# An attention kernel on one Trainium2 core: row maxima written to DRAM head by head, and read back by GpSimd with a stride of four elements

## The chip, the cores and the metric

The kernel runs on one core of a Trainium2 chip. A core has TensorE (PE, matrix products and transposes), VectorE (DVE), ScalarE (ACT), GpSimd (POOL) and SyncE (SP, which here only issues transfers), an on-chip memory SBUF of 128 partitions, an accumulation memory PSUM of eight banks, and sixteen DMA engines that move data between DRAM and SBUF. Each engine works off its own instructions in the order in which they were written; semaphores order the engines among each other.

The metric is the device time of one execution in microseconds (us), as the median of several runs.

## What is computed

One block of a transformer: attention over 16 heads of 8 channels with a bucket term, and a feed-forward network, each followed by a normalization and a residual sum. The input has 16 batches of 512 tokens of 128 channels, in f32.

```
def attention(x, Wq, bq, Wv, bv, hyperplanes):        # B=16, S=512, E=128, H=16
    q = (x @ Wq.T + bq).reshape(B, S, H, 8)
    v = (x @ Wv.T + bv).reshape(B, S, H, 8)
    bits = (concat([q, 1]) @ hyperplanes >= 0)         # 6 bits -> a bucket of 64
    buckets = sum(bits * 2 ** arange(6))
    scores = q @ q.T / sqrt(E)                         # per batch and head, 512 x 512
    same = buckets[:, None] == buckets[None, :]
    attn = softmax(scores * (62 + same), axis=-1)
    return attn @ v

x = x + layernorm(attention(layernorm(x)))
x = x + layernorm(ffn(layernorm(x)))                   # 128 -> 512 -> 512 -> 512 -> 128
```

Queries serve as keys, so scores times coefficient is a symmetric matrix: the maximum of row s is the maximum of column s.

## The kernel before

**Order.** All instructions are put into an order ahead of time by a small planner, `Order` (lines 47 to 187). The kernel is written as generators that yield steps such as `dve(cost, rank, emit)`, `pool(...)`, `act(...)`, `pe(...)` and `dma(kb, rank, emit)`; the planner holds a clock for each engine, and at each moment emits the ready step with the lowest rank. The costs in the code are its estimates in us. Buffers are handed out by `Pool` objects (lines 361 to 374), so a step that needs a buffer is emitted after the step that gives it back. Each engine's queue is then fixed, SP's with the transfers too.

**A head.** There are 16 x 16 = 256 heads j, each with a 512 x 512 matrix of logits, kept in one tile `l` of 128 partitions x 4 x 512. Row s = 128 t + p lies in partition p, part t. The steps are:

- `gather` (L821): three transfers on SP bring ql and qr (the queries, split into three bf16 parts) and bb (the buckets, repeated over all partitions). Four sets of these buffers exist.
- `scores` (L872) and `coeffs` (L889): four products on TensorE (L881) into three PSUM banks, four comparisons of buckets on VectorE (L899).
- `logits` (L913): four instructions on VectorE (L934), each multiplying scores by coefficients into `l` and leaving the maximum of each row in one column of a small tile. There are eleven buffers for `l`.
- `maxima` (L963): the maxima lie with one row in each partition, and are wanted as one line of 512 values in every partition. The tile that took them is one of two tiles `mxpads` of 128 x 32 f32 (lines 322 to 326). VectorE transposes it in blocks of 32 x 32 (L967), SP writes the result to a DRAM tile `md` (L972) in the order of the columns. From the fifth head on, two heads share one such tile, one transpose and one write (`MH = 2`); the first four heads go singly (`SINGLES = 4`).
- `softmax` (L977): SP loads the 512 maxima of the head into each of the 128 partitions (tile `mb`, L984, three buffers). GpSimd subtracts them from all four parts of `l` in one instruction over 2048 elements a partition (L991): here column c of every row has the maximum of row c subtracted, so the matrix becomes the transpose of the softmax's argument. ScalarE takes the exponential in place (L996).
- `attend` (L1040): for each four heads, TensorE multiplies by the values (L1056), which needs the matrix with the summed index in the partitions, hence the subtraction by columns.

Five heads (`BY_ROWS`, j = 3, 7, 11, 15, 19) go another way: ScalarE subtracts the row's maximum from within its exponential (L1007), and TensorE transposes afterwards. They don't use GpSimd, so it subtracts 251 times.

GpSimd also takes small powers for the normalizations (L469, L593), and two scalings of weights (L1369) at the start. The feed-forward network (`ffn`, L1139) of a batch runs among the heads of later batches: its products are L1208, L1252 and L1290, its activations L1196 and L1266 on ScalarE.

Of the kernel before, what the change touches and what calls it, by code (L numbers as in the profile page):

```python
# [13 lines left out]
F32 = mybir.dt.float32  # L14
BF16 = mybir.dt.bfloat16
AF = mybir.ActivationFunctionType
ALU = mybir.AluOpType
# [4 lines left out]
P = 128  # L22
# [168 lines left out]
def tile_lsh_attention_ffn(  # L191
# [20 lines left out]
    nc = tc.nc  # L212
    B, S, E = x.shape
    NH = hyper.shape[1]
    DH = hyper.shape[0] - 1
    H = E // DH
    HID = w1_t.shape[1]
    NT = S // P
    NC = HID // P
    GH = 4  # L220
    NG = H // GH
    Q = P // GH
# [5 lines left out]
    GROUPS = (1, 2, 6, B)  # L228
    LATE = 20
    COLD = 10.0  # L230
    SINGLES = 4
    SCALE = 1.0 / math.sqrt(E)
    AHEAD = 1
    MH = 2
    LB = 11
    BY_ROWS = (3, 7, 11, 15, 19)
    SLOTS = H * NT
# [2 lines left out]
    const = ctx.enter_context(tc.tile_pool(name="const", bufs=1))  # L240
    p1 = ctx.enter_context(tc.tile_pool(name="p1", bufs=1))
    p2 = ctx.enter_context(tc.tile_pool(name="p2", bufs=2))
    ps_b = ctx.enter_context(tc.tile_pool(name="ps_b", bufs=1, space=PSUM))
    dram = ctx.enter_context(tc.tile_pool(name="dram", bufs=2, space=DRAM))

    od = Order()
# [17 lines left out]
        out=hb_sb,  # L264
        in_=hyper[DH].unsqueeze(0).unsqueeze(2).to_broadcast([H, NH, 1]),
# [31 lines left out]
        op=ALU.mult,  # L297
# [16 lines left out]
    for i in range(2):  # L314
# [3 lines left out]
            va[:, :, 0 : H * DA].rearrange("p t (h d) -> p t h d", d=DA)[:, :, :, DH], 1.0  # L318
        )
        vaugs.append(va)  # L320

    mxpads = []
    for i in range(2):
        mp = const.tile([P, Q], F32, name=f"mxpad{i}")
        nc.vector.memset(mp, 0.0)
        mxpads.append(mp)
    bkts = []
    for i in range(2):
        bk = const.tile([H, BR, BP], BF16, name=f"bkt{i}")
# [6 lines left out]
    def pe(cost, rank, emit):  # L336
        return ("op", "PE", cost, emit, rank, None)

    def dve(cost, rank, emit):
        return ("op", "DVE", cost, emit, rank, None)  # L340

    def act(cost, rank, emit, table=None):
        return ("op", "ACT", cost, emit, rank, table)

    def pool(cost, rank, emit):
        return ("op", "POOL", cost, emit, rank, None)

    def dma(kb, rank, emit, held=True, cost=0.35):
        return ("dma", "SP", cost, emit, rank, None, kb, held)

    def get(kind):
        return ("get", kind)

    def wait(event):
        return ("wait", event)

    def events(n):
        return [Event() for _ in range(n)]
# [5 lines left out]
    logit_bufs = Pool("l", LB)  # L364
    row_bufs = Pool("r", 4)
    co_bufs = Pool("co", 4)
    mx_bufs = Pool("mx", 2)
    mb_bufs = Pool("mb", 3)
    row_mx_bufs = Pool("rx", 2)
    h_bufs = Pool("h", 3)  # L370
    x1_bufs = Pool("x1_", 2)
    xnt_bufs = Pool("xntf", 1)
# [11 lines left out]
    def bank(tag, name):  # L384
        return ps_b.tile([P, 512], F32, tag=tag, name=name)
# [525 lines left out]
                od.loose()  # L911

    def logits():  # L913
        pair = []
        for j in range(B * H):
            kl = yield get(logit_bufs)
            by_rows = j in BY_ROWS
            if by_rows:
                kr = yield get(row_mx_bufs)
                mx_, base = p1.tile([P, NT], F32, tag=kr, name=f"mx_{j}"), 0  # L920
            else:
                if not pair:
                    km = yield get(mx_bufs)
                    mx = mxpads[int(km[2:])]
                mx_, base = mx, len(pair) * NT
            l = p1.tile([P, NT, S], F32, tag=kl, name=f"l_{j}")
            for t in range(NT):
                i = j * NT + t
                yield wait(scored[i])
                yield wait(weighed[i])  # L930
                (sp, ks), (co, kc) = sps.pop(i), cos.pop(i)

                def emit(t=t + base, sp=sp, co=co, l=l[:, t, :], mx=mx_):
                    nc.vector.tensor_tensor_reduce(  # L934
                        out=l,
                        in0=co[:, 0:S],
                        in1=sp,
                        scale=1.0,
                        scalar=-3.0e38,
                        op0=ALU.mult,  # L940
                        op1=ALU.max,
                        accum_out=mx[:, t : t + 1],
                    )

                yield dve(0.61, 5, emit)
                od.put(score_banks, ks)
                od.put(co_bufs, kc)
                if t < NT - 1:
                    od.loose()
            od.put(row_bufs, rows.pop(j)[3])  # L950
            ls[j] = l, logit_bufs, kl
            if by_rows:
                od.spawn(softmax_by_rows(j, l, kl, mx_, kr))
            else:
                pair.append((j, l))
                if j < SINGLES or len(pair) == MH or j == B * H - 1:
                    od.spawn(maxima(pair, mx, km))
                    pair = []
            if j % GH == GH - 1:
                od.spawn(attend(j // GH))  # L960
            od.loose()

    def maxima(heads, mx, km):  # L963


        mt = p2.tile([P, Q], F32, tag="mt", name=f"mt_{heads[0][0]}")
        yield dve(0.14, 0, lambda: nc.vector.transpose(mt, mx))  # L967
        od.put(mx_bufs, km)

        md = dram.tile([Q, GH, Q], F32, tag="md", name=f"md_{heads[0][0]}", bufs=4)  # L970
        yield dma(
            16, 0, lambda: nc.sync.dma_start(out=md.rearrange("t k q -> k t q"), in_=mt), cost=0.6  # L972
        )
        for i, (j, l) in enumerate(heads):
            od.spawn(softmax(j, l, md[i * NT : (i + 1) * NT]))

    def softmax(j, l, md):  # L977

        km = yield get(mb_bufs)
        mb = p1.tile([P, S], F32, tag=km, name=f"mb_{j}")  # L980
        yield dma(
            256,
            0,
            lambda: nc.sync.dma_start(  # L984
                out=mb, in_=md.rearrange("t k q -> (t k q)").partition_broadcast(P)
            ),
        )
        yield pool(
            4.52,
            1,  # L990
            lambda: nc.gpsimd.tensor_tensor(  # L991
                l, l, mb.unsqueeze(1).to_broadcast([P, NT, S]), op=ALU.subtract
            ),
        )
        od.put(mb_bufs, km)
        yield act(1.82, 0, lambda: nc.scalar.activation(l, l, AF.Exp, scale=SCALE), "exp")  # L996
        od.set(exped[j])

    def softmax_by_rows(j, l, kl, mx, kr):


        nmx = p1.tile([P, NT], F32, tag="n" + kr, name=f"nmx_{j}")
        yield act(0.22, -5, lambda: nc.scalar.activation(nmx, mx, AF.Copy, scale=-SCALE))

        def weigh():
            for t in range(NT):
                nc.scalar.activation(  # L1007
                    l[:, t, :], l[:, t, :], AF.Exp, bias=nmx[:, t : t + 1], scale=SCALE
                )

        yield act(2.3, 0, weigh, "exp")
        od.put(row_mx_bufs, kr)
        kh = yield get(h_bufs)
        w = p1.tile([P, NT, S], F32, tag=kh, name=f"w_{j}")
        there = events(NT)

        def evict(t, tp, k):
            yield act(0.5, -2, lambda: nc.scalar.copy(w[:, t, :], tp))
            od.put(banks, k)
            od.set(there[t])  # L1020

        for t in range(NT):
            k = yield get(banks)
            tp = bank(k, f"tw_{j}_{t}")

            def turn(t=t, tp=tp):
                for i in range(NT):
                    nc.tensor.transpose(tp[:, ts(i, P)], l[:, i, ts(t, P)], ident)

            yield pe(0.45, 1, turn)  # L1030
            od.spawn(evict(t, tp, k))
        od.put(logit_bufs, kl)
        for e in there:
            yield wait(e)
        ls[j] = w, h_bufs, kh
        od.set(exped[j])
# [373 lines left out]
    with tc.manual_schedule():  # L1410
        for piece in (prep(0), gathers(), scores(), coeffs(), logits(), weights(), inputs(), activity()):
            od.spawn(piece)
        od.run()
# [52 lines left out]
```

## Time and profile before

| | us |
|---|---|
| median of 3 runs | 1368.63 (1368.58 to 1369.19) |
| the profiled execution, its own time | 1371.57 |
| its span, from first to last instruction | 1369.80 |
| first subtraction on GpSimd (L991) starts | 41.45 |
| last subtraction ends | 1295.23 |

The granted clock of TensorE was 0.989 of full speed over the span.

Some groups of instructions, in number, mean duration and the total of their busy time:

| line | engine | what | number | mean ns | busy us |
|---|---|---|---|---|---|
| L934 | DVE | logits and maxima | 1024 | 680 | 662.4 |
| L899 | DVE | coefficients | 1024 | 471 | 451.7 |
| L996 | ACT | exponential | 251 | 1907 | 477.8 |
| L1252 | PE | products of the two middle layers | 1088 | 570 | 494.3 |
| L881 | PE | scores | 1024 | 384 | 357.8 |

Where GpSimd stood idle, and what ended it: waits for the load of mb 41.5 us (20.7 of it before the very first), for the powers' inputs from ScalarE the greater part of the rest.

How to read it: a row of a group names line, engine, operation, the tile written and the tiles read, their shapes, how often it ran, the busy time in us and the mean of one in ns, and behind the bar the idle time of the engine just ahead of it with what ended that. The chain of waits goes back from the last instruction, at each step to what released it. Consecutive instructions overlap a little, so a group's busy time can be less than number times mean.

### The profile page before, as it was taken

Reading aid. Unit: us, or ns where it says so; the run is one execution under the profiler, and the core shown is the slowest. Engines: PE = TensorE matmul, PEld = TensorE weight load, DVE = VectorE, ACT = ScalarE, POOL = GpSimd, SP = SyncE. Lnnn points to the kernel's source line nnn. Section 1 sums busy time; section 2 is a strip of 40 time slices with the busy share of each in tenths; the row PEclk is TensorE's granted clock in tenths of the full one; section 3 lists DMA queues with packets and bytes.
Section 4 is the critical chain, followed back from the end, with each engine's and each line's share of the span. In section 5 each row is a group of like instructions: output and inputs, shape, how many; then the busy total and the mean of one; then the engine's idle time right before and its main releaser. Section 6 shows DMA issues by size and latency. Waiting matters only on the chain.

```text
span 1369.8 us, 21290 instructions
## 1 busy us (share of the span) xinstructions
PE 1316.2 (96%) x6008; PEld 568.3 (41%) x6008; DVE 1234.5 (90%) x3992; ACT 1143.8 (84%) x1665; POOL 1197.4 (87%) x317
## 2 busy tenths in 40 slices
PE   9999999999999999999999999999999999999997
PEld 3344334334443443434344344433443343433466
DVE  4999999799998999999999999999999999999220
ACT  2688888889898898889989798988979898888953
POOL 1398989999899998999989999998999999899810
PEclk9999999899999999999999999999999999999999
DMA  4645454444544545454444545554445545443100
GB/s 135 189 140 154 131 151 138 135 129 134 154 113 128 131 133 142 132 142 134 132 123 128 141 133 144 132 143 116 146 124 139 141 132 140 122 122 116 47 8 8
DMA packets 158867, 174.04 MB, mean 127 GB/s; under 512 B 33821, under 2 KB 117277, under 8 KB 158749
## 3 DMA queue, kind: packets, MB, share of 16 engines
q1 hardware_dynamic: 155937, 169.20, 44.3%
q10 hardware_dynamic: 2811, 3.48, 0.8%
q8 instruction: 48, 0.79, 0.2%
q14 instruction: 71, 0.57, 0.2%
HBM read 153.50 MB, written 19.13 MB: 126 GB/s over the span
## 4 chain that ended last, share of the span: by engine, by line
PE 57%; DVE 24%; POOL 6%; issue 6%; DMA 4%; ACT 3%; SPq 0%; ACTq 0%; POOLq 0%; DVEq 0%
PE hp L1252 25%; PE av L1056 13%; DVE l L934 12%; PE sp L881 10%; DVE co L899 8%; POOL l L991 6%; PE w L1208 3%; DMA mb<-md 2%; PE yp L1290 2%; PE op L1077 2%; DMA bb<-bkd 1%; ACT l L996 1%; PE vp L794 1%; PE activity L1396 1%; DVE h L1178 1%
## 5 line engine op out<-in xcount | busy, mean ns | idle before, releaser
L991 POOL TENSOR_TENSOR l<-l,mb 128x2048 f32<-128x2048 f32 x251 | 1135.6, 4566 | 56.8 <-DMA mb<-md 41.5
L934 DVE CUSTOM_DVE_ANT_0 l<-co,sp 128x512 f32<-128x512 bf16 x1024 | 662.4, 680 | 14.5 <-PE av L1056 11.0
L996 ACT ACTIVATE l<-l 128x2048 f32<-128x2048 f32 x251 | 477.8, 1907 | 23.3 <-POOL l L991 22.1
L1252 PE MATMUL hp<-h,h 128*128 128x512 f32 (+1 forms) x1088 | 494.3, 570 | 0.1
L899 DVE TENSOR_SCALAR co<-bb,bj 128x516 bf16<-128x516 bf16 x1024 | 451.7, 471 | 2.8 <-DMA bb<-bkd 2.8
L881 PE MATMUL sp<-qr,ql 72*128 72x512 bf16 x1024 | 357.8, 384 | 35.6 <-DVE mxpad L934 31.8
L1252 PEld LDWEIGHTS hp<-h,h 128*128 128x128 f32 x1088 | 201.4, 190 | 160.3 <-issue 137.7
L1056 PE MATMUL av<-l,vaug 128*32 128x512 f32 x2008 | 265.1, 605 | 0.0
L881 PEld LDWEIGHTS <-ql 72*128 72x128 bf16 x1024 | 94.6, 98 | 331.8 <-issue 309.6
L1208 PE MATMUL w<-xnt_f,w 128*128 128x512 f32 (+1 forms) x272 | 133.1, 585 | 4.3 <-ACT a L1196 2.6
L996 ACT ACT_TABLE_LOAD x87 | 111.6, 1283 | 1.5
L1056 PEld LDWEIGHTS av<-l,vaug 128*32 128x32 f32 x2008 | 45.7, 109 | 116.6 <-issue 85.2
L1396 PE MATMUL activity<-still 128*128 128x512 bf16 x328 | 88.8, 387 | 1.0 <-DVE still L281 1.0
L934 DVE DVE_READ_ACCUMULATOR2_ANT mxpad<- 128x1 f32 x1004 | 83.0, 83 | 0.0
L1070 ACT COPY avs<-av 128x512 f32<-128x512 f32 x64 | 37.4, 584 | 48.3 <-PE av L1056 48.2
L1266 ACT ACT_TABLE_LOAD x59 | 75.7, 1283 | 1.0
L1208 PEld LDWEIGHTS w<-xnt_f,w 128*128 128x128 f32 x272 | 50.9, 195 | 51.1 <-issue 20.8
L1178 DVE TENSOR_TENSOR h<-w,a 128x512 f32<-128x512 f32 (+1 forms) x68 | 44.2, 656 | 29.4 <-PE w L1208 18.9
L1290 PEld LDWEIGHTS yp<-w,h 128*128 128x128 f32 x512 | 65.7, 193 | 11.3 <-issue 6.7
L1290 PE MATMUL yp<-w,h 128*128 128x128 f32 x512 | 66.5, 277 | 0.0
L469 POOL TENSOR_TENSOR rs_y<-ve_y,mhalf 128x4 f32<-128x4 f32 (+1 forms) x17 | 16.7, 985 | 48.4 <-ACT ve_y L458 47.8
L1266 ACT ACTIVATE h<-hp,h1s 128x512 f32<-128x512 f32 (+1 forms) x68 | 41.8, 660 | 14.9 <-PE hp L1252 14.5
(102 smaller groups left out, 1008.4 us busy)
## 6 DMA issues: line engine op xcount, KB each, us to landing
mb<-md SPq DMA_DIRECT2D x251, 256.0 KB
bb<-bkd SPq DMA_DIRECT2D x256, 130.5 KB
ql<-qd SPq DMA_DIRECT2D x256, 72.0 KB
qr<-qd SPq DMA_DIRECT2D x255, 72.0 KB
qd<-q SPq DMA_DIRECT2D x96, 128.0 KB
xta<-in_L_attn_x_dram SPq DMA_DIRECT2D x16, 256.0 KB
xtr<-in_L_attn_x_dram SPq DMA_DIRECT2D x16, 256.0 KB
xtm<-in_L_attn_x_dram SPq DMA_DIRECT2D x15, 256.0 KB
```

Of the source, the lines that this page charges most:

```text
L881: nc.tensor.matmul(sp, lhsT=ql[:, ts(t, P)], rhs=qr, start=True, stop=True)
L899: nc.vector.tensor_scalar(co, bb.rearrange("p (r c) -> p r c", c=BP)[:, :, 0:BC], bjs[b][:, c : c + 1], float(NBKT - 2), op0=ALU.is_equal, ...
L934: nc.vector.tensor_tensor_reduce(out=l, in0=co[:, 0:S], in1=sp, scale=1.0, scalar=-3.0e38, op0=ALU.mult, op1=ALU.max, accum_out=mx[:, t : ...
L991: lambda: nc.gpsimd.tensor_tensor(l, l, mb.unsqueeze(1).to_broadcast([P, NT, S]), op=ALU.subtract),
L996: yield act(1.82, 0, lambda: nc.scalar.activation(l, l, AF.Exp, scale=SCALE), "exp")
L1056: nc.tensor.matmul(av[k * Q : (k + 1) * Q, :], lhsT=va[:, t, c : c + Q], rhs=ls[gg * GH + k][0][:, t, :], start=(t == 0), stop=(t == NT - 1),)
L1178: lambda: nc.vector.tensor_tensor(h[:, c, cols], g2, a, op=ALU.mult),
L1208: lambda: nc.tensor.matmul(gp, lhsT=w_sb[which][:, 0, ts(c, P)], rhs=xnt[:, cols], start=True, stop=True),
L1252: lambda i=i: nc.tensor.matmul(hp, lhsT=w[:, i, ts(c, P)], rhs=hin[:, i, cols], start=(i == 0), stop=(i == NC - 1),),
L1266: nc.scalar.activation(h[:, c, cols], hp, AF.Gelu, scale=sc[:, c : c + 1])
L1290: nc.tensor.matmul(yp[:, ts(t, E)], lhsT=h[:, i, ts(t, P)], rhs=w_sb["w3"][:, i, :], start=(i == 0), stop=(i == NC - 1),)
L1396: nc.tensor.matmul(bk, lhsT=still, rhs=still.unsqueeze(1).to_broadcast([P, NT, P]), start=start, stop=stop,)
```

## The change

The transpose on VectorE, the padded tiles and the pairing of heads are gone. Each head's maxima, a tile `mx` of 128 x 4 f32 from a pool of six, are written to DRAM as they lie: 16 bytes from each partition, so that DRAM holds the value of row 128 t + p at place 4 p + t. The load of `mb` copies these 512 values into every partition in that order. The subtraction then walks through `l` in order, as k, t, q (its part k, and column 128 t + q), and reads `mb` at 4 q + t: with a step of four elements in the innermost run of 128. The heads that go by rows take their tile of maxima from the same pool.

```
@@ lists of constants and buffers
-    SINGLES = 4
-    MH = 2
-    mxpads = []
-    for i in range(2):
-        mp = const.tile([P, Q], F32, name=f"mxpad{i}")
-        nc.vector.memset(mp, 0.0)
-        mxpads.append(mp)
-    mx_bufs = Pool("mx", 2)
+    mx_bufs = Pool("mx", 6)
-    row_mx_bufs = Pool("rx", 2)
@@ def logits():
-            by_rows = j in BY_ROWS
-            if by_rows:
-                kr = yield get(row_mx_bufs)
-                mx_, base = p1.tile([P, NT], F32, tag=kr, name=f"mx_{j}"), 0
-            else:
-                if not pair:
-                    km = yield get(mx_bufs)
-                    mx = mxpads[int(km[2:])]
-                mx_, base = mx, len(pair) * NT
+            km = yield get(mx_bufs)
+            mx = p1.tile([P, NT], F32, tag=km, name=f"mx_{j}")
...
-            if by_rows:
-                od.spawn(softmax_by_rows(j, l, kl, mx_, kr))
+            if j in BY_ROWS:
+                od.spawn(softmax_by_rows(j, l, kl, mx, km))
             else:
-                pair.append((j, l))
-                if j < SINGLES or len(pair) == MH or j == B * H - 1:
-                    od.spawn(maxima(pair, mx, km))
-                    pair = []
+                od.spawn(softmax(j, l, mx, km))
@@ def maxima, def softmax
-    def maxima(heads, mx, km):
-        mt = p2.tile([P, Q], F32, tag="mt", name=f"mt_{heads[0][0]}")
-        yield dve(0.14, 0, lambda: nc.vector.transpose(mt, mx))
+    def softmax(j, l, mx, km):
+        md = dram.tile([P, NT], F32, tag="md", name=f"md_{j}", bufs=6)
+        yield dma(2, 0, lambda: nc.sync.dma_start(out=md, in_=mx), cost=0.45)
         od.put(mx_bufs, km)
-        md = dram.tile([Q, GH, Q], F32, tag="md", name=f"md_{heads[0][0]}", bufs=4)
-        yield dma(
-            16, 0, lambda: nc.sync.dma_start(out=md.rearrange("t k q -> k t q"), in_=mt), cost=0.6
-        )
-        for i, (j, l) in enumerate(heads):
-            od.spawn(softmax(j, l, md[i * NT : (i + 1) * NT]))
-
-    def softmax(j, l, md):
         km = yield get(mb_bufs)
         mb = p1.tile([P, S], F32, tag=km, name=f"mb_{j}")
         yield dma(
             256,
             0,
             lambda: nc.sync.dma_start(
-                out=mb, in_=md.rearrange("t k q -> (t k q)").partition_broadcast(P)
+                out=mb, in_=md.rearrange("p t -> (p t)").partition_broadcast(P)
             ),
         )
         yield pool(
             4.52,
             1,
             lambda: nc.gpsimd.tensor_tensor(
-                l, l, mb.unsqueeze(1).to_broadcast([P, NT, S]), op=ALU.subtract
+                l.rearrange("p k (t q) -> p k t q", t=NT),
+                l.rearrange("p k (t q) -> p k t q", t=NT),
+                mb.rearrange("p (q t) -> p t q", t=NT).unsqueeze(1).to_broadcast([P, NT, NT, P]),
+                op=ALU.subtract,
             ),
         )
```

The planner's cost of the subtraction, 4.52, is the same in both kernels.

More of the change, by code (lines that the diff above doesn't have):

```diff
@@ L931, in logits, with emit @@
                 (sp, ks), (co, kc) = sps.pop(i), cos.pop(i)
-                def emit(t=t + base, sp=sp, co=co, l=l[:, t, :], mx=mx_):
+                def emit(t=t, sp=sp, co=co, l=l[:, t, :], mx=mx):
                     nc.vector.tensor_tensor_reduce(
@@ L951, in logits @@
             ls[j] = l, logit_bufs, kl
-            if by_rows:
-                od.spawn(softmax_by_rows(j, l, kl, mx_, kr))
-            else:
-                pair.append((j, l))
-                if j < SINGLES or len(pair) == MH or j == B * H - 1:
-                    od.spawn(maxima(pair, mx, km))
-                    pair = []
+            if j in BY_ROWS:
+                od.spawn(softmax_by_rows(j, l, kl, mx, km))
+            else:
+                od.spawn(softmax(j, l, mx, km))
             if j % GH == GH - 1:
@@ L997, in softmax, with softmax_by_rows @@
         od.set(exped[j])
-    def softmax_by_rows(j, l, kl, mx, kr):
-        nmx = p1.tile([P, NT], F32, tag="n" + kr, name=f"nmx_{j}")
+    def softmax_by_rows(j, l, kl, mx, km):
+        nmx = p1.tile([P, NT], F32, tag="n" + km, name=f"nmx_{j}")
         yield act(0.22, -5, lambda: nc.scalar.activation(nmx, mx, AF.Copy, scale=-SCALE))
@@ L1011, in softmax_by_rows @@
         yield act(2.3, 0, weigh, "exp")
-        od.put(row_mx_bufs, kr)
+        od.put(mx_bufs, km)
         kh = yield get(h_bufs)
```

## The prediction

> **What bounds the kernel now.** I first read the busy shares, then the chain of waits, then the busy time in three stretches cut at GpSimd's first and last subtraction, then the groups by line and the issues on SP's queue.
>
> ```profile
> PE 1316.2 (96%) x6008; PEld 568.3 (41%) x6008; DVE 1234.5 (90%) x3992; ACT 1143.8 (84%) x1665; POOL 1197.4 (87%) x317
> ...
> PE 57%; DVE 24%; POOL 6%; issue 6%; DMA 4%; ACT 3%; SPq 0%; ACTq 0%; POOLq 0%; DVEq 0%
> ```
>
> TensorE is ahead with 57% of the chain, but a share of 6% for GpSimd doesn't mean that GpSimd has room. The stretches show that (busy us, instructions in brackets):
>
> ```profile
> core 0: us, PE busy (x) PEld busy (x) DVE busy (x) ACT busy (x) POOL busy (x), PEclk, DMA share, GB/s
> 0.00:41.45 41.45, 38.05 (x156) 16.38 (x157) 23.06 (x82) 14.82 (x49) 5.43 (x13) 0.96 0.51 145
> 41.45:1295.30 1253.85, 1212.41 (x5547) 504.79 (x5546) 1200.76 (x3864) 1092.42 (x1524) 1186.79 (x297) 0.99 0.48 134
> 1295.30:1369.80 74.50, 65.73 (x308) 47.17 (x307) 10.68 (x47) 36.52 (x94) 5.13 (x7) 0.97 0.02 8
> ```
>
> In the middle stretch of 1253.85 us three engines are nearly equal: TensorE is free for 41 us, VectorE for 53, GpSimd for 67. The rows the change touches:
>
> ```profile
> L991 POOL TENSOR_TENSOR l<-l,mb 128x2048 f32<-128x2048 f32 x251 | 1135.6, 4566 | 56.8 <-DMA mb<-md 41.5 <-DVE co L899 9.7 <-DVE mt L967 2.9
> ...
> L967 DVE STREAM_TRANSPOSE mt<-mxpad 128x32 f32<-128x32 f32 x127 | 25.8, 203 | 0.0
> ...
> masks.py:197 POOL MEMSET ident<- 128x128 f32 x1 | 0.2, 205 | 0.3 <-POOLq L1445 0.3
> L273 POOL MEMSET mhalf<- 128x64 f32 x1 | 0.2, 152 | 0.0
> ```
>
> One line, L991, is 1135.6 of GpSimd's 1186.8 us. Whatever is added to one subtraction is paid 251 times, against 67 us of idle time. The two memsets are the only pair on GpSimd that prices a single access to SBUF per element.
>
> **The change, part by part.**
>
> *Removed from VectorE:* 127 transposes of 203 ns, 25.8 us busy, and two memsets of 85 ns at the start. VectorE holds 24% of the chain, so the gain is 6.2 us by that share and at most 25.8 if VectorE alone set the pace. It counts only while GpSimd isn't the bound.
>
> *Writes of maxima on SP's queue:* 127 become 251 (one per head that goes to GpSimd; five heads go by rows as before).
>
> ```profile
> L972 SPq DMA_DIRECT2D md<-mt x127: 549/562/575, 33.6 to 1271.5; - x127
> ...
> L984 SPq DMA_DIRECT2D mb<-md x251: 314/373/1076, 36.9 to 1280.8; - x126
> ```
>
> An issue of the new shape (128 partitions, 16 bytes each) isn't in the trace. By the two rows above it takes 0.373 to 0.562 us, so SP spends 94 to 141 us instead of 71: 22 to 70 more. SP's issues add up to about 740 us (mb 94, md 71, ql 256 x 0.788 = 202, qr 255 x 0.722 = 184, bb 256 x 0.428 = 110, the rest about 80), so some 630 us stand free: I take nothing. Without that cover the 70 us would be the price. In the DMA records a packet of 128 bytes takes 13 ns and one of 24 bytes 7 ns, so 16 bytes cost 7 to 13 ns: nothing for 128 of them on sixteen engines. Each write waits for its head's last maximum, and behind it on SP stand the gathers ql, qr and bb, for which TensorE and VectorE wait. That wait exists today; now it comes for each head, not each pair. A price for it is at worst the 70 us above, in the free case only; a gain is also possible, since the first head of a pair no longer waits a head's time (1253.85 / 251 = 5.0 us) for its partner. This moves latency, not work: nothing.
>
> *The read of the broadcast row,* mb, keeps 256 KB in 251 loads with 2 KB to a partition, contiguous on both sides. Nothing.
>
> *The subtraction.* It still touches 2048 elements in a partition, but mb is read with a step of four f32, 16 bytes, in runs of 128. The trace of before has no strided read on GpSimd, so the cost is bounded from rows. First the runs: the two scalings of weights at L1369 are the same 512 products, once as one run of 512 and once as four of 128 with a repeated second operand, and took 1264 and 1267 ns. Shorter runs cost nothing there; from above, 12 more runs can't each cost more than GpSimd's smallest instruction, 99 ns (a memset of 128x1): 0 to 1.19 us. I take 0, because that row is the nearest. Then the stride. Lower end: 0; on VectorE, writing the projected values in runs of 8 with gaps between (L802) takes 681 ns, and a plain product of that size (L1321) 679. A gain is excluded: the same elements in a pattern no simpler. Upper end: the slope of this operation is (4562 - 1266) / (2048 - 512) = 2.146 ns an element for two reads and a write; if mb is a third of that, and 16 bytes that held four wanted values now hold one, three more such thirds are 3 x 0.715 x 2048 = 4.39 us. Between: each element of mb costs one more access by itself, priced by the memset slope (205 - 152) / (128 - 64) = 0.83 ns, so 1.70 us, a subtraction of 6.27 us. I take this one: it is the row of the same engine and memory for a single access per element, and lies near the doubling of mb's third (0.715 x 2048 = 1.46) and of half the slope (2.20).
>
> [...]
>
> *The sum.* 251 x 1.70 = 425.7 us. Of GpSimd's 67.1 us idle I keep 16.5, the waits while the pipeline fills (3.97, 0.78 and 8.73 us up to 69 us, 2.97 at 96 us). The other 50.6 us are waits for data that come earlier than needed once GpSimd paces everything: eleven logit buffers stand before it, and three rows of maxima, of which two are full while the third loads. In the first head that load took 4.56 us from issue to use (36.89 to 41.45), which two subtractions of 6.27 us cover; without that cover it is 4.56 us a head. The load of mb waits on SP for its buffer, with the gathers behind it, a wait of 72.6 us in total now and longer then; it is hidden by the same two subtractions. On ScalarE the exponentials wait for GpSimd with the feed-forward's activations behind them, and then TensorE: both follow at GpSimd's pace. So 41.45 + (1186.79 + 425.7) + 16.5 + 74.5 = 1744.9 us of span. The profiled execution took 1371.57 with a span of 1369.80, 1.77 around it, and stands 2.94 above the median of 1368.63. 1744.9 + 1.77 - 2.94 = **1744 us**.
>
> **Rivals.**
>
> *A. The stride is free.* For: the row of VectorE, and the equal pair at L1369. Against: neither is a strided read on GpSimd. GpSimd stays at 4.57 us, and of VectorE's gain 6 to 26 us come through; TensorE's 41 us of idle time limit it, so about 10: 1359 us (1343 to 1380, where the planner's new order or SP's 70 us eat it). This ends on the other side.
>
> *B. The stride costs, but part hides behind the other streams,* 0.2 to 0.85 us, half of 1.70. It decides from 50.6 / 251 = 0.20 us on. 1369 + 0.65 x 251 = 1532 at its end, 1450 in its middle. For: the operation already takes 2.146 ns an element, more than two single accesses. Against: no row shows that reads and the write overlap.
>
> *C. The full price of fetching 16 bytes for 4:* 4.39 us, 251 x 4.39 = 1102, so 1744 + 1102 - 426 = 2420 us.
>
> *D. It doesn't do what it says,* in that the pattern is too deep and the subtraction goes out in four pieces. Each has a fixed part of 1.266 - 512 x 0.002146 = 0.167 us, three more make 0.50 us or 126 us in all: 1744 + 126 = 1870 us. For: three nested steps instead of two. Against: operands on GpSimd here show three counts. It lies in the forecast's own range.
>
> **How the numbers follow.** Forecast with D 0.70, A 0.13 (of it 0.10 faster, 0.02 the same, 0.01 slower), B 0.12, C 0.05. A change within 0.2%, about 2.7 us, couldn't be told from none. Faster 0.10, same 0.03 (0.01 of B's lower edge goes there), slower 0.87. The forecast's own range goes from 1532 (half the price) to 1.70 + 1.19 = 2.89 us a subtraction, 1744 + 1.19 x 251 = 2043. It holds 0.68; to reach 0.8 nearly all of B comes in, down to 1380, and A and C stay outside: 1380 to 2040.
>
> **What would show it.** Right: L991 still 251 times, at 6.0 to 6.9 us, with a minimum and a median close together; GpSimd at 95% or more of the stretch between its first and last subtraction; VectorE and TensorE falling to some 75% there; GpSimd at the head of the chain; no L967; 251 writes of maxima. Wrong: L991 at 4.57 us (A), or at 6.3 us with GpSimd's idle time not shrinking, which would mean that the loads of mb come too late. TensorE has 1212 us of work for a stretch that would last 1629: only a granted clock under about 0.74 would make it the bound.

## The result, and the profile after

| | before | changed |
|---|---|---|
| median, us | 1368.91 (4 runs) | 1627.52 (1625.89 to 1630.22, 4 runs) |
| ratio to the kernel before | | 1.1887, 95% interval 1.1865 to 1.1908 |
| span of the profiled execution, us | 1369.8 | 1625.7 |
| mean granted clock of TensorE | 0.989 | 0.941 |

The changed kernel is slower by 18.9%. Its busy shares and its chain of waits, to be held against the same two lines of before:

```profile
PE 1409.0 (87%) x5987; PEld 585.1 (36%) x5987; DVE 1235.5 (76%) x3863; ACT 1145.5 (70%) x1663; POOL 1485.0 (91%) x317
...
POOL 48%; issue 19%; PE 14%; DVE 7%; DMA 7%; ACT 4%; SPq 1%; POOLq 0%; ACTq 0%; DVEq 0%
```

GpSimd went from 6% to 48% of the chain, and TensorE from 57% to 14%. VectorE's busy time is the same to 1 us although its transposes are gone (without the stride it is 1225.6 us, in a run further down). The three stretches, cut again at GpSimd's first and last subtraction (stretch, its length, then busy us and instructions of each engine, granted clock, DMA share, GB/s):

```profile
0.00:42.19 42.19, 39.07 (x161) 16.84 (x162) 24.33 (x82) 14.49 (x48) 5.45 (x14) 1.00 0.51 140
42.19:1527.40 1485.21, 1280.06 (x5442) 508.95 (x5440) 1195.68 (x3722) 1075.12 (x1483) 1472.52 (x296) 0.94 0.46 112
1527.40:1625.70 98.30, 89.86 (x387) 59.29 (x386) 15.46 (x60) 55.94 (x133) 7.07 (x9) 0.97 0.02 9
```

In the middle stretch GpSimd is busy for 1472.5 of 1485.2 us: 12.7 us idle where there were 67.1. The last stretch has grown from 74.5 to 98.3 us; GpSimd has only 7 us of work there, and without the stride this stretch is as long (99.7 us, further down). The row of the subtraction, then its durations in ns (least, median, greatest) in the kernel before and in the changed one, and the two transfers on SP's queue:

```profile
L962 POOL TENSOR_TENSOR l<-l,mb 128x2048 f32<-128x2048 f32 x251 | 1432.7, 5907 | 33.3 <-DMA mb<-md 24.1 <-DVE mx L917 9.2
```

```profile
L991 POOL TENSOR_TENSOR l<-l,mb x251: 4510/4562/4683, 41.5 to 1290.7; 128x2048 f32<-128x2048 f32 x126
```

```profile
L962 POOL TENSOR_TENSOR l<-l,mb x251: 5538/5867/6675, 42.2 to 1521.4; 128x2048 f32<-128x2048 f32 x126
```

```profile
L948 SPq DMA_DIRECT2D md<-mx x251: 319/362/1672, 31.6 to 1501.4; - x126
...
L955 SPq DMA_DIRECT2D mb<-md x251: 314/320/2381, 36.2 to 1509.8; - x126
```

It is one instruction a head, 251 as before. Its mean went from 4566 to 5907 ns; its group is busy for 1432.7 us, which is 5.71 a subtraction, because the end of one overlaps the start of the next. Before, all 251 lay between 4510 and 4683 ns; now they spread from 5538 to 6675. An issue of the new write takes 362 ns.

### The profile page after: what moved, and what is told of

The parts are those of the page before. It is cut to its first block, busy times and chain, and to the rows that moved or that the text cites. A ratio compares the mean times of both kernels' runs of the same rounds, so it can differ in the third digit from the quotient of the medians.

```text
span 1625.7 us, 21432 instructions
## 1 busy us (share of the span) xinstructions
PE 1409.0 (87%) x5987; PEld 585.1 (36%) x5987; DVE 1235.5 (76%) x3863; ACT 1145.5 (70%) x1663; POOL 1485.0 (91%) x317
## 4 chain that ended last, share of the span: by engine, by line
POOL 48%; issue 19%; PE 14%; DVE 7%; DMA 7%; ACT 4%; SPq 1%; POOLq 0%; ACTq 0%; DVEq 0%
POOL l L962 44%; PE hp L1226 5%; DMA mb<-md 5%; DVE l L917 3%; DVE co L890 2%; ACT l L970 2%; PE av L1030 2%; PE w L1182 2%; PE sp L872 2%; PE yp L1264 1%; POOL rs_o L460 1%; POOL rs_f L460 1%; POOL rs_y L460 1%; DMA bb<-bkd 1%; POOL rs_x L584 1%
## 5 line engine op out<-in xcount | busy, mean ns | idle before, releaser
L962 POOL TENSOR_TENSOR l<-l,mb 128x2048 f32<-128x2048 f32 x251 | 1432.7, 5907 | 33.3 <-DMA mb<-md 24.1
L1226 PE MATMUL hp<-h,h 128*128 128x512 f32 (+1 forms) x1088 | 521.2, 594 | 19.9 <-ACT h L1240 10.5
L872 PE MATMUL sp<-qr,ql 72*128 72x512 bf16 x1024 | 375.9, 399 | 113.8 <-DVE mx L917 107.9
L1030 PE MATMUL av<-l,vaug 128*32 128x512 f32 x2008 | 291.8, 622 | 16.4 <-ACT l L970 13.7
L1226 PEld LDWEIGHTS hp<-h,h 128*128 128x128 f32 x1088 | 210.8, 199 | 228.6 <-issue 170.2
L1182 PE MATMUL w<-xnt_f,w 128*128 128x512 f32 (+1 forms) x272 | 148.2, 642 | 19.5 <-ACT a L1170 15.4
L917 DVE DVE_READ_ACCUMULATOR2_ANT mx<- 128x1 f32 x1024 | 83.8, 82 | 0.0
L468 DVE TENSOR_SCALAR nm_y<-su_y,rs_y 128x1 f32<-128x1 f32 x64 | 9.3, 206 | 69.7 <-POOL rs_y L460 69.7
L468 DVE TENSOR_SCALAR nm_o<-mv_o,rs_o 128x1 f32<-128x1 f32 x64 | 9.3, 207 | 58.8 <-POOL rs_o L460 58.8
```

The source lines that it names most:

```text
L872: nc.tensor.matmul(sp, lhsT=ql[:, ts(t, P)], rhs=qr, start=True, stop=True)
L917: nc.vector.tensor_tensor_reduce(out=l, in0=co[:, 0:S], in1=sp, scale=1.0, scalar=-3.0e38, op0=ALU.mult, op1=ALU.max, accum_out=mx[:, t : ...
L962: lambda: nc.gpsimd.tensor_tensor(l.rearrange("p k (t q) -> p k t q", t=NT), l.rearrange("p k (t q) -> p k t q", t=NT), mb.rearrange("p (q ...
L1030: nc.tensor.matmul(av[k * Q : (k + 1) * Q, :], lhsT=va[:, t, c : c + Q], rhs=ls[gg * GH + k][0][:, t, :], start=(t == 0), stop=(t == NT - 1),)
L1182: lambda: nc.tensor.matmul(gp, lhsT=w_sb[which][:, 0, ts(c, P)], rhs=xnt[:, cols], start=True, stop=True),
L1226: lambda i=i: nc.tensor.matmul(hp, lhsT=w[:, i, ts(c, P)], rhs=hin[:, i, cols], start=(i == 0), stop=(i == NC - 1),),
```

## The experiments

Runs that subtract the maxima of other columns, or leave out part of attention's sum, have a smaller scale in the exponential, so that it stays finite; their expectations say so. The first run here is their control. The stride alone, the steps of two, three and eight, the short runs and the run with fewer products were executed once each; kernels that were executed several times scatter by up to 6 us, the version that writes single elements by 21.

### The control: the exponential's scale alone

```
-    nc.scalar.activation(l, l, AF.Exp, scale=SCALE)
+    nc.scalar.activation(l, l, AF.Exp, scale=SCALE / 64)
```

> The changed kernel with nothing changed but the exponential's scale, a 64th: the control for the runs that carry it. If the numbers in the tiles don't matter for the time, 1622 to 1632 us with a median subtraction of 5.87 us. If they do, it takes 1595 to 1602 us, as the run with a step of eight, and the subtractions over 6.2 us go away: then the runs with that scale are to be read against this one.

Measured: 1626.8 us (ratio 1.1879, 1.1856 to 1.1902), the same as the changed kernel. But its median subtraction was recorded at 5.61 us, not 5.87, with the same busy time on GpSimd (1483.4 against 1485.0 us):

```profile
L962 POOL TENSOR_TENSOR l<-l,mb x251: 5516/5610/6210, 42.1 to 1522.4; 128x2048 f32<-128x2048 f32 x126
```

So the recorded durations of single strided subtractions shift from one execution to another while the pace stays; below I compare least durations, distances from start to start, and busy times and stretches of whole runs.

### The stride alone, in the kernel before

```
-    l, l, mb.unsqueeze(1).to_broadcast([P, NT, S]), op=ALU.subtract
+    l.rearrange("p k (t q) -> p k t q", t=NT),
+    l.rearrange("p k (t q) -> p k t q", t=NT),
+    mb.rearrange("p (q t) -> p t q", t=NT).unsqueeze(1).to_broadcast([P, NT, NT, P]),
+    op=ALU.subtract,
```

> The kernel before with nothing changed but the pattern in which the subtraction reads mb: a step of four elements in runs of 128. Transpose, padded tiles and pairs stay. The maxima subtracted are those of other columns, and the exponential's scale is a 64th, so that it stays finite. Theory (the stride is the whole price): the subtraction takes a median of 5.8 to 5.95 us, 5.5 at the least, and the run takes 1610 to 1650 us, as the changed kernel does. Rival (the small writes and the single heads share in the loss): the subtraction is still slow, but the run stays under 1600 us. Rival (the slow subtraction comes from another cause, such as the maxima's tiles): it takes 4.57 us and the run 1369.

Measured: 1598.0 us. Its subtractions and its stretches:

```profile
L991 POOL TENSOR_TENSOR l<-l,mb x251: 5519/5751/6414, 39.9 to 1517.0; 128x2048 f32<-128x2048 f32 x126
```

```profile
39.90:1522.80 1482.90, 1307.51 (x5552) 523.94 (x5551) 1214.43 (x3864) 1097.70 (x1526) 1466.42 (x297) 0.95 0.41 113
1522.80:1596.20 73.40, 64.67 (x306) 46.78 (x304) 10.66 (x47) 35.38 (x93) 5.13 (x7) 0.97 0.02 8
```

The middle stretch is that of the changed kernel to 2.3 us, with the transposes, the padded tiles and the pairs still there. So the stride makes 229 of the 259 us. The other 29.5 us are mostly in the last stretch, which here is 73.4 us and in the changed kernel 98.3. The run came out under 1600 us, as the rival expected, and its median of 5.75 us just under the theory's 5.8: the stride is nearly the whole price, but not all of it. The rest is traced further down, mostly to the planner's order.

### All of the change but the stride

```
-    l.rearrange("p k (t q) -> p k t q", t=NT),
-    l.rearrange("p k (t q) -> p k t q", t=NT),
-    mb.rearrange("p (q t) -> p t q", t=NT).unsqueeze(1).to_broadcast([P, NT, NT, P]),
+    l, l, mb.unsqueeze(1).to_broadcast([P, NT, S]),
```

> The changed kernel with mb read contiguously, as before; maxima of other columns are subtracted, and the exponential's scale is a 64th. Everything else of the change stays: no transpose, one write a head. Theory: the subtraction is back at 4.55 to 4.6 us, and the run takes 1343 to 1369 us, since VectorE has 25.8 us less to do. Rival (writes of 16 bytes and single heads cost): slower than 1372 us.

Measured: 1380.4 us, ratio 1.0072 (1.0051 to 1.0092), with the subtraction back at a mean of 4577 ns. Without its stride the change still costs 0.7%. Its stretches:

```profile
41.80:1281.40 1239.60, 1192.79 (x5440) 495.01 (x5439) 1185.84 (x3722) 1070.19 (x1482) 1185.79 (x296) 0.98 0.55 134
1281.40:1381.10 99.70, 91.27 (x393) 60.08 (x391) 15.46 (x60) 57.12 (x134) 7.09 (x10) 0.98 0.02 9
```

The heads are done 14 us sooner (1239.6 for 1253.9 us), and the last stretch takes 25 us more (99.7 for 74.5), with 91 us of TensorE's work in it for 66 before. The theory (1343 to 1369 us) missed, and the rival's time came, though its cause isn't shown by this. Nor are the 14 us VectorE's gain: TensorE has 19.6 us less to do in the middle stretch and 25.5 more behind it, so work has moved behind the last head.

### Steps of two, three and eight elements, and short runs without a step

```
# step 2 (8 bytes), two runs of 256
+    mb.rearrange("p (q t) -> p t q", t=2).unsqueeze(1).to_broadcast([P, NT, 2, S // 2]),
# step 3 (12 bytes), one run of 128, sixteen times
+    mb[:, 0 : 3 * P].rearrange("p (q t) -> p t q", t=3)[:, 0, :].unsqueeze(1).to_broadcast([P, NT * NT, P]),
# step 8 (32 bytes), eight runs of 64
+    mb.rearrange("p (q t) -> p t q", t=8).unsqueeze(1).to_broadcast([P, NT, 8, S // 8]),
# contiguous, runs of 64 with gaps between
+    mb.rearrange("p (t b q) -> p t b q", t=NT, b=2)[:, :, 0, :].unsqueeze(1).to_broadcast([P, 2 * NT, NT, S // NT // 2]),
```

Expected for the step of two:

> The changed kernel with mb read in two runs of 256 with a step of two elements, 8 bytes; maxima of other columns, the exponential's scale a 64th. If the price grows with the step: between 4.57 and 5.9 us, some 5.0, and GpSimd is the bound at 1420 to 1460 us. If it is one more access for any element that isn't next to the last: 5.8 us, 1610 us. [...]

For the step of three:

> The changed kernel with mb read with a step of three elements, 12 bytes, the same run of 128 sixteen times; maxima of other columns, the exponential's scale a 64th. Measured so far: step of one 4.57 us, of two 4.63, of four 5.87 (5.54 at the least). Theory (a price for each element that lies more than 8 bytes from the last): as with four, 5.5 us at the least and a run of 1600 us or more. Rival (a price that grows with the bytes passed over): about 5.1 to 5.3 us, some 1470 to 1530 us. Rival (free as long as the next element is within 16 bytes, the price only from 16 on): 4.65 us, 1375 to 1390 us.

For the step of eight:

> The changed kernel with mb read with a step of eight elements, 32 bytes, in runs of 64; maxima of other columns, the exponential's scale a 64th. Theory (one price for each element fetched by itself, whatever the distance): 5.5 us at the least, a median near 5.9, and 1610 to 1645 us, as with a step of four. Rival (the price follows the bytes passed over): over 6.5 us and over 1800 us.

For the short runs:

> The changed kernel with mb read contiguously in 32 runs of 64 elements with gaps between (half of the columns, each used twice); maxima of other columns, the exponential's scale a 64th. Theory (stride, not runs): 4.55 to 4.65 us and 1343 to 1375 us. Rival (each start of a run costs): with 28 starts more than before against 12 more in the changed kernel, 28/12 of its 1.3 us or more, 7 us or more a subtraction and over 1850 us.

Measured, with the run without a stride as the zero:

| step | least, us | above step 1 | mean, us | run, us |
|---|---|---|---|---|
| 1 | 4.505 | 0 | 4.577 | 1380.4 |
| 1, in 32 runs of 64 | 4.512 | 0.01 | 4.566 | 1376.6 |
| 2 (8 bytes) | 4.582 | 0.08 | 4.636 | 1384.0 |
| 3 (12 bytes) | 5.001 | 0.50 | 5.137 | 1491.5 |
| 4 (16 bytes), the changed kernel | 5.538 | 1.03 | 5.907 | 1627.5 |
| 8 (32 bytes) | 5.521 | 1.02 | 5.842 | 1596.2 |

Three of these from their traces, the zero, and steps of three and of eight:

```profile
L962 POOL TENSOR_TENSOR l<-l,mb x251: 4505/4572/4688, 41.8 to 1276.8; 128x2048 f32<-128x2048 f32 x126
```

```profile
L962 POOL TENSOR_TENSOR l<-l,mb x251: 5001/5135/5271, 42.8 to 1385.5; 128x2048 f32<-128x2048 f32 x126
```

```profile
L962 POOL TENSOR_TENSOR l<-l,mb x251: 5521/5874/6202, 41.5 to 1488.8; 128x2048 f32<-128x2048 f32 x126
```

Runs cost nothing: 32 starts are as fast as 4 (4.512 and 4.505 us at the least). (This run is over the 1375 us expected of it, as the zero itself is.) The price is that of the step, and it isn't a cliff with one height: a step of two costs 0.08 us, a step of three pays half of the full price (0.50 us), four pays 1.03 us, and eight no more than four (1.02 us). With a step of two the subtraction took 4.64 us on average, under the 5.0 and the 5.8 us that were expected, and the run's 1384.0 us are under both times too. A price that grows evenly from a step of two to one of four would be 0.56 us at three, by an estimate halfway between 0.08 and 1.03; 0.50 was measured. What makes the price, no run shows. My theory of one price beyond 8 bytes missed the step of three. There the rival, a price by the bytes passed over, was met (5.14 us, 1491.5 us); with eight it wasn't (expected over 6.5 us).

The step of eight ran 31 us shorter than that of four, with the same least duration, and below what was expected of it: its middle stretch took 1453.0 us for 1485.9 in the control. The next run and the distances behind it show where these us lie.

### Fewer products beside the subtractions

```
     for k in range(GH):
+        if t:
+            continue
...
-            stop=(t == NT - 1),
+            stop=True,
```

> The changed kernel with a quarter of the products of weights and values (the first of the four parts alone, so three quarters of attention's sum are left out; the exponentials' scale is a 64th). In the changed kernel a strided subtraction with none of these products beside it takes a median of 5.76 us, and 6.13 with over 1.8 us of them. Theory (TensorE's reads of f32 tiles slow the strided reads): the median falls from 5.87 to 5.70 to 5.78 us, few subtractions are over 6.0, and the run gets 20 to 35 us shorter, 1590 to 1607 us. Rival (the spread comes from what runs at the same time as those products, such as the write of a group's result or the loads): the median stays at 5.85 us or above, and GpSimd's middle stretch keeps its 1485 us.

Measured: 1601.0 us, 26 less than the control with the same scale. The middle stretch of this run, and that of the control:

```profile
40.80:1502.10 1461.30, 1173.39 (x3933) 514.33 (x3932) 1195.18 (x3723) 1074.93 (x1483) 1446.58 (x296) 0.88 0.47 113
```

```profile
42.10:1528.00 1485.90, 1284.75 (x5442) 511.62 (x5440) 1195.95 (x3721) 1075.46 (x1483) 1470.91 (x296) 0.93 0.45 112
```

GpSimd has 24.3 us less to do with 1536 of TensorE's products of weights and values gone, though its own instructions are the same, and its idle time in the stretch is too (14.7 us for 15.0). So these products slow the subtractions with a step of four. The criterion by the median (5.58 us here) tells nothing, since the control's is 5.61. In the changed kernel's trace the 129 subtractions with none of these products beside them have a median of 5.76 us, and the 74 with over 1.8 us of them 6.13; in the kernel before the same division gives 4.55 and 4.58.

The distance from one subtraction's start to the next one's is steadier than the recorded duration. Where GpSimd has nothing between the two and doesn't idle, the traces give these medians in us (number of subtractions in brackets):

| step | none of these products beside it | over 1.8 us of them |
|---|---|---|
| 1 | 4.497 (91) | 4.545 (56) |
| 2 | 4.572 (99) | 4.616 (56) |
| 3 | 5.078 (110) | 5.138 (55) |
| 4, the changed kernel | 5.537 (107) | 5.893 (52) |
| 4, the control | 5.535 (109) | 5.918 (53) |
| 8 | 5.498 (105) | 5.566 (61) |

Beside these products a subtraction with a step of four takes 0.36 to 0.38 us longer, and one with any of the other steps only 0.04 to 0.07. That is where most of the 31 us lie by which the step of eight is shorter (an estimate: the 74 such subtractions of the changed kernel times 0.29 us are 21 us); the run without three quarters of the products was made with a step of four alone. The reason that I had expected, TensorE's reads of f32 tiles in SBUF, isn't shown: the products of the middle layers read f32 tiles from SBUF as well, and of the changed kernel's subtractions with no product of weights and values beside them, the 62 with over 1.5 us of middle-layer products are 5.544 us apart and the 32 with none 5.534. Why it is these products and the step of four stays open.

### The order, with the subtraction's true cost

```
-            4.52,
+            5.7,
```

> The changed kernel with the planner told a cost of 5.7 us for the subtraction in place of 4.52; everything is computed as in the reference, and only the order of the instructions differs. Theory (some 25 us of the loss are the order, which leaves feed-forward work of the last batches behind the last subtraction): the stretch after the last subtraction falls from 98 us to 66 to 76, and the run takes 1595 to 1607 us. Rival (the stretch is what it is, whatever the order): 1622 us and more.

Measured: 1594.3 us, ratio 1.1641 (1.1619 to 1.1664). Its last two stretches:

```profile
41.60:1525.90 1484.30, 1322.70 (x5611) 543.95 (x5610) 1193.29 (x3736) 1113.55 (x1535) 1472.44 (x297) 0.91 0.47 112
1525.90:1594.00 68.10, 50.41 (x262) 40.21 (x260) 10.72 (x47) 33.85 (x88) 5.12 (x7) 0.89 0.02 8
```

GpSimd's work is the same 1472.4 us. The run came out just under the expected 1595. Only the last stretch fell, from 98.3 to 68.1 us, and TensorE's work in it from 89.9 to 50.4: the planner, told the truth, puts the feed-forward products of the last batches among the heads. With that the changed kernel is as fast as the stride alone in the kernel before (1598.0 us), so of the change's other parts no loss is left that stands out of the scatter. The chain of waits of this run shows little of GpSimd:

```profile
PE 56%; DVE 23%; DMA 6%; issue 6%; POOL 5%; ACT 2%; SPq 2%; ACTq 0%; POOLq 0%; DVEq 0%
```

Yet GpSimd is busy for 99% of the middle stretch. Here as in the kernel before, a small share of the chain doesn't mean that an engine has room.

### The kernel before without its transposes, in its own order

```
-        mt = p2.tile([P, Q], F32, tag="mt", name=f"mt_{heads[0][0]}")
-        yield dve(0.14, 0, lambda: nc.vector.transpose(mt, mx))
+        yield dve(0.14, 0, lambda: None)
...
-    nc.sync.dma_start(out=md.rearrange("t k q -> k t q"), in_=mt)
+    nc.sync.dma_start(out=md.rearrange("t k q -> k t q"), in_=mx)
```

> The kernel before without its 127 transposes on VectorE, in exactly its own order: the padded tile is written to DRAM as it lies, in pairs, the same 16 KB, and mb is read contiguously. The maxima subtracted are other values, and the exponential's scale is a 64th. The changed kernel's order without the stride came to 1380 us, 0.7% over the kernel before, with the middle stretch 14 us shorter and the last one 25 us longer. Theory (those 12 us are the order alone, and VectorE's 25.8 us are worth something): the last stretch stays at 73 to 76 us, and the run takes 1350 to 1364 us. Rival (TensorE is the bound, and VectorE's relief is worth nothing in any order): 1366 to 1371 us. Rival (the two padded tiles, now held until the write has read them, make VectorE wait): over 1372 us.

Measured: 1367.4 us (11 runs, beside 15 of the kernel before at 1369.6), ratio 0.9983 (0.9974 to 0.9992). Without the transposes the run is some 2 us shorter where the order stays. VectorE's busy time fell by only 10.0 us (from 1234.5 to 1224.5), not by the 25.8 that the transposes' own durations add up to, since instructions overlap in the record (in the kernel before the durations of VectorE's instructions add up to 1541.9 us, its busy time is 1234.5). The rival's time (1366 to 1371 us) came. That TensorE is the bound agrees with its 1209.7 busy us of 1248.2; no run tried it by itself. The last two stretches, cut at 41.45 us as before (the first subtraction starts at 40.3 here):

```profile
41.45:1289.60 1248.15, 1209.69 (x5541) 504.17 (x5540) 1190.00 (x3736) 1091.60 (x1523) 1184.79 (x297) 0.99 0.50 134
1289.60:1365.70 76.10, 67.30 (x312) 47.91 (x310) 10.67 (x47) 37.04 (x94) 5.12 (x7) 0.97 0.02 7
```

The last stretch stays at about its length, 76.1 us. Against this run, the 13 us of the change without its stride come with the other order; the single writes and loads changed with it and weren't tried by themselves.

### Two versions without transpose and stride

The first writes the maxima in the columns' order, in pieces of one element:

```
-    md = dram.tile([P, NT], F32, tag="md", name=f"md_{j}", bufs=6)
+    md = dram.tile([NT, P], F32, tag="md", name=f"md_{j}", bufs=6)
...
-    nc.sync.dma_start(out=md, in_=mx)
+    nc.sync.dma_start(out=md.rearrange("t p -> p t"), in_=mx, allow_slow_non_contiguous=True)
```

> The changed kernel, but each head's maxima are written to DRAM in the columns' order, element by element (512 pieces of 4 bytes), so that mb is read contiguously; everything is computed as in the reference. Theory: the subtraction takes 4.57 us, and the run takes what the changed kernel takes without its stride, 1377 to 1384 us. Rival (element-wise writes take long on the queue or in landing): 1390 us and more, with waits of GpSimd for mb growing by over 20 us. Rival (better than the kernel before, because VectorE has less to do): under 1366 us.

Measured: 2410.6 us, ratio 1.7577 (1.7521 to 1.7634). GpSimd's subtractions are fast (mean 4529 ns), but SP's own waits (us in total, times, longest) begin with the first line here; the second is the same wait in the changed kernel:

```profile
SPq L962 <- DMA md<-mx: 1054.6, 178, 10.5
```

```profile
SPq L955 <- DMA md<-mx: 45.0, 47, 2.9
```

The load of a head waits on SP 5.9 us on average for the write of 512 pieces of 4 bytes to land, with the gathers behind it, and GpSimd's waits for mb grew from 41.5 us in the kernel before to 897.6: the first rival's outcome. The issue itself takes 378 ns in the median, where that of 128 pieces of 16 bytes took 362. The waits on SP come to about the 1030 us by which this run exceeds the one without a stride. What makes the landing long isn't shown by these records.

The second takes other rows for the parts of a head, so that the maxima lie in order from the start:

```
-    sp, lhsT=ql[:, ts(t, P)], rhs=qr
+    sp, lhsT=ql.rearrange("k (p t) -> k t p", t=NT)[:, t, :], rhs=qr
-    lhsT=bits[:, ts(t, P)]
+    lhsT=bits.rearrange("r (p t) -> r t p", t=NT)[:, t, :]
-    lhsT=xnt[:, ts(t, P)]
+    lhsT=xnt.rearrange("e (p t) -> e t p", t=NT)[:, t, :]
-    nc.tensor.transpose(tp[:, ts(i, P)], l[:, i, ts(t, P)], ident)
+    nc.tensor.transpose(tp.rearrange("q (p i) -> q i p", i=NT)[:, i, :], l[:, i, :].rearrange("p (q t) -> p t q", t=NT)[:, t, :], ident)
...
+    l, l, mb.unsqueeze(1).to_broadcast([P, NT, S]),
```

> A version meant to have neither transpose nor stride: part t of a head takes rows 4p + t, not 128t + p, so the maxima as they lie in DRAM are in the columns' order already, and the subtraction reads mb contiguously. What is strided in its place is the weights that TensorE loads for scores, buckets and values. Everything is computed as in the reference. Theory (as the run without a stride): the subtraction 4.57 us, 1374 to 1384 us. Rival (strided weights load slower, and TensorE is at 96%): the load of 128x72 bf16 weights goes from 98 ns to 130 or more, and the run is over 1390 us. Better than the kernel before only if the stretch after the last subtraction stays under 85 us: 1350 to 1366 us.

Measured: 1391.6 us, ratio 1.0162 (1.0148 to 1.0176). The weight loads of scores and of values, in the kernel before and in this version:

```profile
L881 PEld LDWEIGHTS <-ql 72*128 72x128 bf16 x1024 | 94.6, 98 | 331.8 <-issue 309.6 <-DMA mb<-md 3.4 <-DMA out_dram<-y 3.4
...
L794 PEld LDWEIGHTS vp<-wv_sb,xnt_a 128*128 128x128 f32 x128 | 16.4, 192 | 3.6 <-issue 3.1
```

```profile
L876 PEld LDWEIGHTS <-ql 72*128 72x128 bf16 x1024 | 111.9, 117 | 340.7 <-issue 301.1 <-DMA bb<-bkd 11.7 <-DMA mb<-md 9.7
...
L785 PEld LDWEIGHTS vp<-wv_sb,xnt_a 128*128 128x128 f32 x128 | 31.3, 326 | 3.1 <-PE op L1061 0.9 <-issue 0.9 <-PE hp L1236 0.2
```

They went from 98 to 117 ns (bf16, a step of 8 bytes) and from 192 to 326 (f32, 16 bytes). That is 1024 x 19 + 128 x 134 ns = 37 us more on loads by these means, and the run is 11 us over the one without a stride. That this is what costs the 11 us is argued, not shown: other reads and writes became strided with it, such as those of the transposes. The run is over the rival's 1390 us, with scores' loads below its 130 ns. Among the versions that do the whole work the kernel before stays the fastest.

## Why the prediction was right

Forecast were 1744 us and a bound on GpSimd; 1627.5 us came, inside the forecast's own range. By its steps:

- **The mechanism held.** 251 instructions in one piece, GpSimd busy for 99% of its middle stretch and first in the chain, as forecast. The stride alone, put into the kernel before, gives 1598 us.
- **Three of the forecast's marks were missed.** L991 was to take 6.0 to 6.9 us and took 5.91 on average; its least and median duration were to lie close together and lie 0.33 us apart; VectorE and TensorE were to fall to some 75% of the middle stretch and fell to 81% and 86% (from 96% and 97%).
- **The price of the stride was over-sized.** The term was 1.70 us a subtraction, 425.7 us in all. GpSimd's work in the middle stretch grew by 1472.5 - 1186.8 = 285.7 us, 1.14 a subtraction: 1.04 from start to start with no product of weights and values beside it (5.537 - 4.497). The rest, 0.10 a subtraction or 25 us in all, is of the size of the slowing by these products, which the forecast didn't have. The step that failed is the assumption that a strided element costs one more access by itself, priced by two memsets, which only write (0.83 ns); it cost 0.50 ns (1.03 us / 2048). Why less, no run shows.
- **The runs of 128 at nothing** were right: 32 runs of 64 take 4.57 us.
- **Idle time** was taken as 16.5 us and is 12.7. The loads of mb were covered as expected: the waits of GpSimd for them are 24.1 us, of which 22.8 stand ahead of the first subtraction.
- **The last stretch was taken over unchanged,** 74.5 us, and is 98.3. The diff also changes the planner's order, and I had argued every engine's queue but not what the new order leaves behind the last head. This made the sum 23.8 us too small. Rival A did name the new order, as a loss without saying where.
- **Together:** 1744.9 - 140.0 (price) - 3.8 (idle) + 23.8 (last stretch) + 0.7 (start) = 1625.6 us of span, measured 1625.7. The two large errors have opposite signs, so the total is 119 us too high where the price alone was 140; that they partly cancel is luck.
- **SP's queue at nothing** held: an issue of the new write takes 362 ns, below the lower bound of 373. The wait of the mb loads for their buffers grew from 72.6 to 388.9 us, and GpSimd's waits don't show it (us in total, times, longest; before, then two lines of the changed kernel):

```profile
SPq L984 <- POOL l L991: 72.6, 63, 4.1
```

```profile
SPq L955 <- POOL l L962: 388.9, 197, 5.5
```

```profile
POOL l L962 <- DMA mb<-md: 24.1, 3, 22.8
```

- **Rival A,** the free stride, has a counterpart without the stride: 1380 us, not 1359, the upper end of its range. VectorE's relief is worth 2 us in the same order, not 10, and the new order costs more than that. Rival A itself is out, since the stride isn't free. **Rivals B and C** are out by their sizes (0.20 to 0.85 and 4.39 us, where 1.03 to 1.14 were measured). B's idea, that part of the price hides behind the other streams, isn't excluded by that. **Rival D** is out by the single instruction.

## What to carry to other kernels

When an engine has one dominant instruction and little idle time, multiply any doubt about that instruction by its count before anything else; here 1.14 us times 251. For a subtraction like this one, whose second operand GpSimd reads as f32 from SBUF, keep that operand's step at one or two elements (0 and 0.08 us here). When a planner makes the order, a change of steps or costs also changes what is left behind the last long stage: look at that stretch by itself, and give the planner the measured cost, which was worth 33 us here (1627.5 to 1594.3).

## What was not expected of the hardware

- Beside over 1.8 us of TensorE's products of weights and values the subtraction with a step of four takes 0.36 to 0.38 us longer, and those with steps of one, two, three and eight 0.04 to 0.07. With three quarters of these products left out, GpSimd had 24 us less to do.
- So a step of 32 bytes is faster under load than one of 16, by 31 us in the run, though their least durations are the same (5.52 and 5.54 us).
- 512 pieces of 4 bytes made a write on whose landing SP waited 178 times, 5.9 us on average, where the same 2 KB in 128 pieces of 16 bytes, in the changed kernel, made it wait 47 times for 1.0 us (45.0 us in all).
- TensorE's granted clock was 0.989 in the kernel before, 0.941 in the changed one, 0.910 with the true cost, 0.886 with fewer products and 0.807 with the 4-byte pieces. It doesn't simply follow TensorE's busy share, which was 87% in the changed kernel and 89% with the true cost. Its products of the middle layers (128x512) took 596, 622 and 600 ns in the first three.
